# Group statistics and the channel gate inside the attention stream: blockwise transposes on VectorE in place of one-column matmuls

## The chip, the cores and the metric

The kernel runs on one core of a Trainium2 chip. Its engines each work through a queue of their own in order: TensorE (PE, with its weight loads shown apart as PEld), VectorE (DVE), ScalarE (ACT), GpSimd (POOL) and SyncE (SP, which issues DMAs here). The metric is device time in microseconds (us) for one execution.

## The reference

The input is x of shape (4, 64, 96, 96). Layer 0 normalizes x in 32 groups of two channels, runs an attention whose weights are sigmoids (no softmax), adds the residual, and multiplies each channel by a gate. Layer 1 normalizes again and applies a spectral convolution.

```python
def _gn(v, G=32, eps=1e-5):            # groups of C/G = 2 channels
    g = v.reshape(B_, G, C_ // G, H_, W_)
    m, s = mean(g, (2, 3, 4)), var(g, (2, 3, 4))
    return (g - m) / sqrt(s + eps)

# layer 0, on u = _gn(x):
energy = einsum('bcn,bcm->bnm', Q, K);  att = sigmoid(energy)
out = einsum('bcm,bnm->bcn', V, att) + u
mlp = lambda f: relu(f @ ca_w1.T) @ ca_w2.T      # 64 -> 4 -> 64
scale = sigmoid(mlp(mean(out)) + mlp(max(out)))
x = x + out * scale
# layer 1: low modes of rfft2(_gn(x)) times complex weights, irfft2, plus x
```

## The kernel before

**Layout.** One image is a tile `xs[p]` of 128 partitions by 4608 columns: partition 64h + c holds channel c of the upper (h = 0) or lower (h = 1) half of the picture. A group of two channels therefore lies in four partitions: c, c+1, 64+c, 64+c+1.

**The stream.** The attention of all four images is one long stream of 5184 tiles. A tile is 128 keys by 512 queries: an energy matmul (`energies`, L551) writes one PSUM bank, ScalarE takes the sigmoid into SBUF (`sigmoids`, L572), and a value matmul (`attend`, L589) adds the result to an accumulator bank. An image has 9 query blocks of 144 tiles each; when a block ends, VectorE adds the accumulator to `xs` and takes sums and maxima (L595, L597).

Tiles go in bursts. In round t TensorE does the energies of burst t+1, then the values of tiles whose sigmoids are done; ScalarE does the sigmoids of burst t+1 in two instructions, of three or four banks and the rest. PSUM has 8 banks: one accumulates, seven hold a burst. A round at a block's edge needs both accumulators, and so has a burst of six.

**Side work** is placed by a planner that runs while the kernel is built (L801 to L879), and it writes out the order on TensorE, VectorE and ScalarE by hand:

- `alone[t]`: a step with its own small matmul. It takes the free accumulator bank, so the burst planned in that round has six tiles instead of seven (`few = crossing or t in alone`, L865). It stands between the energies and the values on TensorE, and ahead of the sigmoids on ScalarE's queue.
- `together[t]`: a step that borrows banks of the burst just read (the projections `values_of`, L460, and the way back from the spectrum).
- `ends[t]`: VectorE work or DMA issues at the end of a round. The steps of a round that comes just before an edge are put off until after it (`put_off`, L909).
- `follow(own, step, wait, since)` adds a step to a chain that is handed out in order: `own` True makes it `alone`, None puts it in `ends`, a number in `together`; `wait` is the least number of rounds after the step before it.

**The three places that the change touches:**

1. `stats_of(p)` (L599) for the images p = 1, 2, 3 while image p-1 is attended: nine `bn_stats`, `bn_aggr` (`first`), and then two matmuls against the constant `pav`, which averages over the four partitions of a group: the mean (`shared`, L154), and the variance with the spread of the means (`third`, L165). `second` and `third` are `alone` in the rounds three after the edges m = 4 and m = 5 (L817). GpSimd then raises to the power -1/2 (L168).
2. `after(p)` (L612), the gate of image p, begins at the edge where its attention ends: `means` in `ends`, `hidden` (two matmuls with `w1`, L629 and L630) and `gates` (a matmul with `w2`, L636, a sum on VectorE, L639, and a sigmoid on ScalarE, L640) `alone`, two rounds apart.
3. `stats_steps(p)` (L282), the same statistics for layer 1 of images 0 to 2: two `alone` rounds in the chain after the last `along_w`.

That is 18 `alone` rounds. The chain also holds 9 + 3 + 16 others (`along_w`, `along_h`, `mixing`) that the change leaves.

At the end of round t = edge and in the next ones VectorE also has the last projections of the next image (L487, L477, then its splits), which TensorE needs to be read from PSUM, and copies of its keys (`kT<-stage`, L523), which wait for DMAs issued by GpSimd (L521) six rounds before.

Of the kernel before, what the change touches and what calls it, by code (L numbers as in the profile page):

```python
# [33 lines left out]
F32 = mybir.dt.float32  # L34
# [6 lines left out]
P = 128  # L41
# [6 lines left out]
KW = 16  # L48
# [24 lines left out]
QK = 4 * C8  # L73
FIRST = {"wq": P, "wk": P, "wv": C + 2 * C8, "pav": P, "bq": 1, "bk": 1, "low": 2, "nhalf": 1,
         "bv": P, "bqk": 2 * C8}
SECOND = {"w1": R, "w2": P, "fw": 2 * KW, "fh": 4 * KH, "gh": 2 * H, "gw": 4 * W}
PLACE, _at = {}, 0
for _name, _n in {**FIRST, **SECOND}.items():
    PLACE[_name] = slice(_at, _at + _n)
# [12 lines left out]
def tile_kernel(ctx: ExitStack, tc: tile.TileContext, x, cst, late, spec, out):  # L92
# [41 lines left out]
    def group_stats(stats, bank, name):  # L134


        mv = small.tile([P, 2], F32, tag=f"mv_{name}", name=f"mv_{name}", bufs=1)
        mr = small.tile([P, 2], F32, tag=f"mr_{name}", name=f"mr_{name}", bufs=1)
        t = small.tile([P, 1], F32, tag=f"t_{name}", name=f"t_{name}", bufs=1)
        d = small.tile([P, 1], F32, tag=f"d_{name}", name=f"d_{name}", bufs=1)  # L140

        def first():
            nc.vector.bn_aggr(mv, stats.rearrange("p s k -> p (s k)"))

        def second():
            shared()
            offset()
            spread_out()

        pm = []  # L150

        def shared():
            pm.append(bank(f"pm_{name}"))
            nc.tensor.matmul(pm[0][:, 0:1], pav, mv[:, 0:1], start=True, stop=True)  # L154

        def offset():
            nc.vector.tensor_copy(mr[:, 0:1], pm[0][:, 0:1])
            nc.vector.tensor_tensor(d, mv[:, 0:1], mr[:, 0:1], ALU.subtract)

        def spread_out():  # L160
            nc.vector.scalar_tensor_tensor(t, d, d, mv[:, 1:2], ALU.mult, ALU.add)

        def third():
            pv = bank(f"pv_{name}")
            nc.tensor.matmul(pv[:, 0:1], pav, t, start=True, stop=True)  # L165
            ve = small.tile([P, 1], F32, tag="ve", name=f"ve_{name}")
# [5 lines left out]
        return mr, [first, second, third], mv  # L172

    def normalize(dst, src, mr):
        nc.vector.tensor_scalar(dst, src, mr[:, 0:1], mr[:, 1:2], ALU.subtract, ALU.mult)
# [64 lines left out]
    class Hidden(Mixing):  # L240
# [39 lines left out]
                    self.xd[s].rearrange("(k w) (h n c) -> n w h k c", k=4, n=NSQ, c=SQ)[n])  # L280

        def stats_steps(self, p):  # L282
            mr, steps, _ = group_stats(self.stats[p], self.bank, f"l1_{p}")
            return steps + [lambda: self.spread(p, mr)]

        def spread(self, p, mr):
# [117 lines left out]
    with tc.tile_pool(name="work", bufs=1) as work, \  # L404
# [16 lines left out]

        def bank_a(name):
            return banks[:, spare[0], :]

        projected = [None]
        attended = [None]
# [172 lines left out]
        def stats_of(p):  # L599

            stats = small.tile([P, NBLK, 6], F32, tag=f"stats0_{p}", bufs=1, name=f"stats0_{p}")
            mr, steps, mv = group_stats(stats, bank_a, f"l0_{p}")
# [9 lines left out]
        def after(p):  # L612

            f = small.tile([P, 2], F32, tag=f"f{p}", bufs=1, name=f"f_{p}")
            top = small.tile([C, 1], F32, tag=f"top{p}", bufs=1, name=f"top_{p}")
            hid = small.tile([R, 2], F32, tag=f"hid{p}", bufs=1, name=f"hid_{p}")
            gate = small.tile([P, 1], F32, tag=f"gate{p}", bufs=1, name=f"gate_{p}")

            def means():
                tot = small.tile([P, 1], F32, tag="tot", name=f"tot_{p}")  # L620
                nc.vector.tensor_reduce(f[:, 1:2], maxs[p], AX.X, ALU.max)
# [3 lines left out]
                nc.vector.tensor_scalar(f[:, 0:1], tot, 1.0 / HALF, None, ALU.mult)  # L625

            def hidden():
                ph = bank_a(f"ph_{p}")
                nc.tensor.matmul(ph[:R, 1:2], named("w1", C), f[:C, 1:2], start=True, stop=True)  # L629
                nc.tensor.matmul(ph[:R, 0:1], named("w1"), f[:, 0:1], start=True, stop=True)  # L630
                nc.vector.tensor_scalar(hid[:, 0:1], ph[:R, 0:1], 0.5, 0.0, ALU.mult, ALU.max)
                nc.vector.tensor_scalar(hid[:, 1:2], ph[:R, 1:2], 0.0, None, ALU.max)

            def gates():
                pg = bank_a(f"pg_{p}")
                projected[0] = nc.tensor.matmul(pg[:, 0:2], named("w2", R), hid,  # L636
                                                start=True, stop=True)
                gsum = small.tile([P, 1], F32, tag="gsum", name=f"gsum_{p}")
                nc.vector.tensor_reduce(gsum, pg[:, 0:2], AX.X, ALU.add)  # L639
                nc.scalar.activation(gate, gsum, AF.Sigmoid)  # L640

            return gate, [means, hidden, gates], f

        def warm(s, n=NB // 2):

# [38 lines left out]
        def end(t, step):  # L684
            ends.setdefault(t, []).append(step)
# [17 lines left out]
        def follow(own, step, wait=1, since=0):  # L703

            chain.append((own, step, wait, since))
# [7 lines left out]
                nc.gpsimd.dma_start(w, spec[NSLOT + i])  # L713

        l1 = Hidden(bank_a, lambda dst, src: nc.vector.tensor_copy(dst, src), work)  # L715
        l1.banks = lambda n: banks[:, spare[0]:spare[0] + n, :]
        places = {}

# [22 lines left out]

        def second_layer(p, first):

            gate, steps, _ = after(p)
            end(first, steps[0])
            for step in steps[1:]:
                follow(True, step, 2)
            apart = APART if p < HIDDEN - 1 else APART_LAST
            end(first + 3, lambda: l1.fetch(p, 0))
            for s in range(NSTRIP):  # L750
                end(first + 7 + apart * s, lambda s=s: l1.result(p, s, gate))
                end(first + 9 + apart * s, lambda s=s: l1.turned(p, s))
            for m in range(NSTRIP // 2):
                follow(True, lambda m=m: l1.along_w(p, m), 1, 15 + apart * (2 * m + 1))
            stats = l1.stats_steps(p)
            follow(None, stats[0])
            for step in stats[1:3]:
                follow(True, step, 2)
            follow(None, lambda: (stats[3](), home(p)), 2)
            follow(True, lambda: l1.along_h(p), 2)  # L760
            if p < HIDDEN - 1:
                return

            def room():
# [36 lines left out]
        while len(done) < len(sizes):  # L801
# [6 lines left out]
            if crossing:  # L808
                edges.add(t)
                p, m = (n - 1) // NBLK + 1, (n - 1) % NBLK + 1  # L810
                for i in range(4):
                    if p < B and m >= 6 and 4 * (m - 6) + i < NBLK:
                        end(t + 2 + i, stats0[p][1][4 * (m - 6) + i])
                    if p < B and 4 * (m - 1) + i <= NBLK:
                        end(t + 2 + i, stats0[p][0][4 * (m - 1) + i])
                if p < B and m in (4, 5):
                    alone[t + 3] = stats0[p][0][NBLK + m - 3]  # L817
                if p == B and 3 <= m < 6:
                    for s in (2 * m - 6, 2 * m - 5):
                        end(t + 2, lambda s=s: bring(s))  # L820
# [319 lines left out]
def _constants(l0):  # L1140
# [15 lines left out]
    def put(name, what, rows=slice(0, P)):  # L1156
        a[rows, PLACE[name]] = what
# [8 lines left out]
    for b in range(2):  # L1166
# [8 lines left out]
            a[:, at:at + C8] = l0[w][None, :]  # L1175
        a[rows, PLACE["w1"]] = l0["ca_w1"].T
        a[:R, PLACE["w2"].start + b * C:PLACE["w2"].start + (b + 1) * C] = l0["ca_w2"].T
    put("bv", np.tile(l0["bv"], 2)[None, :])
    put("pav", np.kron(np.ones((2, 2)), np.kron(np.eye(C // 2), np.full((2, 2), 0.25))))

# [65 lines left out]
```

## Time and profile before

| | |
|---|---|
| median of three runs | 3021.2 us (3020.45 to 3021.38) |
| the profiled execution | 3020.43 us, of which the span of its instructions is 3018.7 us |
| PE busy | 3000.9 us (99%) |
| ACT busy | 2406.6 us (80%) |
| DVE busy | 335.8 us (11%), 814 instructions |
| POOL busy | 145.0 us (5%) |
| granted TensorE clock | 0.999 |

The stream begins 18.9 us after the span's start; its last burst begins at 2957.0 us. What follows is the tail: layer 1 of the last image. In a timeline, a group of L551 matmuls begins a burst, and the time to the next such group is the length of the round. An energy matmul is one record; a value matmul and the small ones are two. Values are taken in pairs of tiles and halves of pairs, so that seven tiles of values show as x16 of L589 and six as x12 or x16.

### The profile page before, as it was taken

The page shows a single profiled execution, that of the slowest core. Times are in us where ns is not written, and L with a number is a line of the kernel's source. Part 1 is how long each engine was busy: PE and PEld are TensorE (multiplying, and loading weights), DVE is VectorE, ACT ScalarE, POOL GpSimd, SP SyncE. Part 2 cuts the span into 40 slices and gives each one's busy share as a digit, 9 for nine tenths or more (in the row PEclk, how much of TensorE's full clock was granted, in tenths as well). Part 3 has the DMA queues.
Part 4 walks back from the last instruction along what each step waited for, and adds up shares of the span by engine and source line. Part 5 has one row for each costly group of instructions (what it writes and reads, how often), then busy time and mean ns, then how long its engine had stood idle before and what let it go on. Part 6 is the DMA issues. An engine that isn't in the chain of part 4 may idle for free.

```text
span 3018.7 us, 44581 instructions
## 1 busy us (share of the span) xinstructions
PE 3000.9 (99%) x19360; PEld 1091.3 (36%) x19360; DVE 335.8 (11%) x814; ACT 2406.6 (80%) x1539; POOL 145.0 (5%) x295
## 2 busy tenths in 40 slices
PE   9999999999999999999999999999999999999998
PEld 3333333333333333333333333333333333333334
DVE  4100000002111000001311000000221110100104
ACT  5888888887887888888788888888788777777783
POOL 1100000004000000001300000000310000000000
PEclk9999999999999999999999999999999999999999
DMA  4000000002230000001322000000243243312224
GB/s 167 20 4 4 4 4 4 4 2 56 68 77 17 4 4 4 4 5 23 82 69 72 4 4 4 4 3 2 44 109 98 77 158 86 55 47 64 67 93 153
DMA packets 157267, 133.96 MB, mean 44 GB/s; under 512 B 118960, under 2 KB 123120, under 8 KB 156784
## 3 DMA queue, kind: packets, MB, share of 16 engines
q1 hardware_dynamic: 145152, 110.06, 13.5%
q0 software_dynamic: 11344, 19.69, 2.2%
q8 instruction: 152, 2.49, 0.3%
q10 hardware_dynamic: 576, 1.38, 0.1%
q14 instruction: 43, 0.35, 0.0%
HBM read 91.53 MB, written 38.73 MB: 43 GB/s over the span
## 4 chain that ended last, share of the span: by engine, by line
PE 98%; DVE 1%; DMA 0%; ACT 0%; issue 0%; SPq 0%; POOL 0%; DVEq 0%; ACTq 0%
PE banks L589 78%; PE banks L551 17%; PE banks L470 1%; PE banks L215 1%; PE banks L394 0%; PE pv L215 0%; PE banks L300 0%; PE banks L366 0%; DMA x<-in_x_dram 0%; PE banks L328 0%; ACT at L572 0%; PE pa L1007 0%; DVE xt L997 0%; PE banks L436 0%; DVE x L180 0%
## 5 line engine op out<-in xcount | busy, mean ns | idle before, releaser
L572 ACT ACTIVATE at<-banks 128x2048 f32<-128x2048 f32 (+1 forms) x1505 | 2388.9, 1638 | 548.2 <-PE banks L551 535.8
L589 PE MATMUL banks<-at,vT 128*64 128x512 f32 (+1 forms) x11780 | 2406.6, 548 | 0.0
L589 PEld LDWEIGHTS banks<-at,vT 128*64 128x64 f32 x11780 | 773.8, 136 | 1352.3 <-issue 1297.5
L551 PE MATMUL banks<-q,kT 32*128 32x512 f32 x5040 | 543.0, 452 | 0.3 <-ACT at L572 0.3
L551 PEld LDWEIGHTS banks<-q,kT 32*128 32x128 f32 x5040 | 223.6, 182 | 453.0 <-issue 331.4
L595 DVE SCALAR_TENSOR_TENSOR x<-banks,x 128x512 f32<-128x512 f32 x36 | 24.9, 692 | 1663.4 <-PE banks L589 1663.4
L521 POOL DMA_DIRECT2D stage<-qk x256 | 125.7, 499 | 937.7 <-DMA qk<-turned 927.1
L168 POOL TENSOR_TENSOR mr_l<-ve_l,cs 128x1 f32<-128x1 f32 x7 | 3.9, 556 | 1288.7 <-DVE ve_l L167 1288.7
L398 DVE TENSOR_TENSOR x<-banks,x 128x768 f32<-128x768 f32 x18 | 17.2, 958 | 212.3 <-PE banks L394 212.3
L470 PEld LDWEIGHTS banks<-cs,x 64*64 64x64 f32 x1152 | 22.6, 135 | 27.2 <-ACT at L572 25.6
L487 DVE TENSOR_TENSOR u<-banks,cs 128x128 f32<-128x128 f32 x35 | 10.2, 291 | 191.0 <-PE banks L470 191.0
L739 POOL DMA_DIRECT2D w_early<-in_spec_dram x12 | 6.4, 542 | 518.5 <-PE banks L394 357.7
L470 PE MATMUL banks<-cs,x 64*64 64x80 f32 (+1 forms) x1152 | 28.3, 236 | 0.0
L477 DVE TENSOR_TENSOR vT<-banks,cs 128x256 f32<-128x256 f32 x72 | 26.9, 415 | 0.0
L715 DVE COPY ae<-banks 128x512 f32<-128x512 f32 x9 | 6.2, 692 | 174.8 <-PE banks L300 128.8
L597 DVE TENSOR_REDUCE maxs<-x 128x1 f32<-128x512 f32 x36 | 24.7, 686 | 1.2
L715 DVE COPY ws<-banks 128x512 f32<-128x512 f32 x16 | 11.1, 692 | 116.8 <-PE banks L215 116.8
L603 DVE BATCH_NORM_STATS2 stats<-x 128x6 f32<-128x512 f32 x36 | 23.3, 681 | 4.3 <-DMA x<-in_x_dram 4.3
L180 DVE SCALAR_TENSOR_TENSOR x<-x,gate,old 128x768 f32<-128x768 f32 x18 | 18.2, 1009 | 17.5 <-DMA old<-in_x_dram 17.5
L508 DVE STREAM_TRANSPOSE turned<-t 128x384 f32<-128x384 f32 (+1 forms) x35 | 19.9, 568 | 1.4 <-DVE t L506 0.3
L551 PE MATMUL banks<-q_first,kT 32*128 32x512 f32 x144 | 16.6, 463 | 2.7 <-ACT at L572 1.8
L523 DVE CAST kT<-stage 128x256 fp32r<-128x256 f32 x64 | 16.0, 287 | 24.3 <-DMA stage<-qk 24.1
(144 smaller groups left out, 402.0 us busy)
## 6 DMA issues: line engine op xcount, KB each, us to landing
ws<-in_spec_dram SPq DMA_DIRECT2D x32, 512.0 KB
q<-qk SPq DMA_DIRECT2D x280, 32.0 KB
stage<-qk POOLq DMA_DIRECT2D x256, 32.0 KB, 1.9
out_dram<-x SPq DMA_DIRECT2D x20, 384.0 KB
x<-in_x_dram SPq DMA_DIRECT2D x9, 768.0 KB
old<-in_x_dram SPq DMA_DIRECT2D x18, 384.0 KB
x1d<-x SPq DMA_DIRECT2D x18, 384.0 KB
xd<-old SPq DMA_DIRECT2D x18, 384.0 KB
```

The costliest lines, as they stand in the source:

```text
L180: nc.vector.scalar_tensor_tensor(xs[p][:, cols], xs[p][:, cols], gate, old, ALU.mult, ALU.add)
L215: self.last = nc.tensor.matmul(pv[bass.ts(g, 32), :].rearrange("q (n k o) -> q n k o", n=SIDE, o=C)[:, :, k, :], self.ut[:, at:at + 32], s ...
L470: projected[0] = nc.tensor.matmul(pp[bass.ts(e, P // 2), b, 2 * a + h, :width], src[rows, a, h, bass.ts(e, P // 2)], named("wv")[rows, :wi ...
L477: nc.vector.tensor_tensor(vTs[p % 2][:, 8 * s:8 * s + 8, :].rearrange("p (a h b) m -> p b a h m", h=2, b=2)[:, b], pp[:, b, :, :C].rearran ...
L508: nc.vector.transpose(turned[:, k:].rearrange("p k a (m h) -> p (k a) h m", h=2), t[:, k:].rearrange("p k a h m -> p (k a) h m").bitcast(F32))
L521: nc.gpsimd.dma_start(come[bass.ts(r, QK), :], split[p][s // 2][:, r // 2, bass.ts(s % 2, NB // 2)])
L551: nc.tensor.matmul(banks[:, bank_of(i), :], kT[r:r + 32, i % TILES // 8, i // 4 % 2, :], ask[i // TILES][r:r + 32, :], start=True, stop=True)
L572: nc.scalar.activation(at[:, of:of + n, :], banks[:, bank:bank + n, :], AF.Sigmoid)
L589: attended[0] = nc.tensor.matmul(acc[half, cols], vTs[n // NBLK % 2][:, j, :], at[:, place(2 * pair + b), cols], start=(j == 0), stop=(j = ...
L595: nc.vector.scalar_tensor_tensor(blk, acc, 1.0, blk, ALU.mult, ALU.add, accum_out=sums[p][:, m:m + 1])
L597: mark[0] = nc.vector.tensor_reduce(maxs[p][:, m:m + 1], blk, AX.X, ALU.max)
L603: each = [lambda s=s: nc.vector.bn_stats(stats[:, s, :], xs[p][:, bass.ts(s, NB)]) for s in range(NBLK)]
```

## The change

The steps listed above lose their matmuls. In the stream, `group_stats` is replaced by `group_stats_across`: `first` as before; `halves` brings the lower half's 64 partitions over and averages the two halves, then transposes a 64x64 patch in 32x32 blocks, so that channels lie along the row; `neighbours` averages even and odd channels there, writes the result to both, and transposes back; `third` copies the result to both halves. The gate's `after(p, True)` does its two small products as elementwise products with constants laid out for it (`w1r`, `w2r`, 36 more columns of the constant tile), sums along rows, and transposes. All scratch space is one `ae` tile (two buffers, shared with `along_w` and others).

The steps are put in `ends`, one a round, instead of `alone`. The statistics of layer 0 come right after the last `bn_stats`. The first image's statistics (before the stream) and the last image's gate and layer-1 statistics (after it) stay as they were.

```diff
+    def group_stats_across(stats, name, scratch):
+        def halves():
+            of, line, _, _ = places()
+            other, gap = place(7 * SQ, 7 * SQ + 2, False), place(7 * SQ + 2, 7 * SQ + 3, False)
+            nc.vector.memset(of, 0.0)
+            nc.vector.tensor_copy(other, mv[C:])
+            nc.vector.tensor_tensor(of[:, :, 0], mv[:C], other, ALU.add)
+            nc.vector.tensor_tensor(gap, mv[:C, 0:1], other[:, 0:1], ALU.subtract)
+            nc.vector.tensor_scalar(of[:, :, 0], of[:, :, 0], 0.5, None, ALU.mult)
+            nc.vector.tensor_scalar(gap, gap, 0.5, None, ALU.mult)
+            nc.vector.scalar_tensor_tensor(of[:, 1, 0:1], gap, gap, of[:, 1, 0:1], ALU.mult, ALU.add)
+            nc.vector.transpose(line, of)
+        def neighbours():
             ...   (even and odd columns averaged, nine instructions, the last a transpose)
+        def third():
+            for half in range(2):
+                rows = bass.ts(half, C)
+                nc.vector.tensor_copy(mr[rows, 0:1], line[:, 0, 0:1])
+                nc.vector.tensor_scalar(ve[rows], line[:, 1, 0:1], GN_EPS, None, ALU.add)
+            nc.gpsimd.tensor_tensor(mr[:, 1:2], ve, nhalf, ALU.pow)
+        return mr, [first, halves, neighbours, third], mv
...
         def stats_steps(self, p):
-            mr, steps, _ = group_stats(self.stats[p], self.bank, f"l1_{p}")
+            mr, steps, _ = group_stats_across(self.stats[p], f"l1_{p}", self.scratch)
...
+            def pooled():
+                means()
+                nc.vector.tensor_copy(top, f[C:, 0:1])
+                nc.vector.tensor_tensor(top, f[:C, 0:1], top, ALU.add)
+                nc.vector.tensor_scalar(f[:C, 0:1], top, 0.5, None, ALU.mult)
+                wide, lines = pairs(0), pairs(2 * SQ)
+                nc.vector.tensor_copy(wide, f[:C].unsqueeze(2).to_broadcast([C, 2, SQ]))
+                nc.vector.transpose(lines, wide)
+            def squeezed():
             ...   (product with w1r, sums, relu, spread over 128 partitions, transpose: 11 instructions)
+            def excited():
+                nc.vector.tensor_tensor(line[:, :R], line[:, :R], named("w2r"), ALU.mult)
+                nc.vector.tensor_reduce(gsum, line[:, :R], AX.X, ALU.add)
+                nc.scalar.activation(gate, gsum, AF.Sigmoid)
...
         def second_layer(p, first):
-            gate, steps, _ = after(p)
-            end(first, steps[0])
-            for step in steps[1:]:
-                follow(True, step, 2)
+            gate, steps, _ = after(p, True)
+            for i, step in enumerate(steps):
+                end(first + i, step)
...
-            stats = l1.stats_steps(p)
-            follow(None, stats[0])
-            for step in stats[1:3]:
-                follow(True, step, 2)
-            follow(None, lambda: (stats[3](), home(p)), 2)
+            for step in l1.stats_steps(p):
+                follow(None, step)
+            follow(None, lambda: home(p))
...
-                    if p < B and 4 * (m - 1) + i <= NBLK:
+                    if p < B and 4 * (m - 1) + i < len(stats0[p][0]):
                         end(t + 2 + i, stats0[p][0][4 * (m - 1) + i])
-                if p < B and m in (4, 5):
-                    alone[t + 3] = stats0[p][0][NBLK + m - 3]
```

More of the change, by code (lines that the diff above doesn't have):

```diff
@@ L75 @@
          "bv": P, "bqk": 2 * C8}
-SECOND = {"w1": R, "w2": P, "fw": 2 * KW, "fh": 4 * KH, "gh": 2 * H, "gw": 4 * W}
+SECOND = {"w1": R, "w2": P, "w1r": SQ, "w2r": R, "fw": 2 * KW, "fh": 4 * KH, "gh": 2 * H, "gw": 4 * W}
 PLACE, _at = {}, 0
@@ L172, in group_stats, with place, places, first @@
         return mr, [first, second, third], mv
+    def group_stats_across(stats, name, scratch):
+        mv = small.tile([P, 2], F32, tag=f"mv_{name}", name=f"mv_{name}", bufs=1)
+        mr = small.tile([P, 2], F32, tag=f"mr_{name}", name=f"mr_{name}", bufs=1)
+        room = []
+        def place(first, last, pair=True):
+            if not room:
+                room.append(scratch(name))
+            of = room[0][:C, first:last]
+            return of.rearrange("p (k n) -> p k n", k=2) if pair else of
+        def places():
+            return [place(0, 2 * SQ), place(2 * SQ, 4 * SQ), place(4 * SQ, 6 * SQ),
+                    place(6 * SQ, 7 * SQ, False)]
+        def first():
+            nc.vector.bn_aggr(mv, stats.rearrange("p s k -> p (s k)"))
+        def halves():
[10 more added lines that the diff above has]
+        def neighbours():
+            _, line, both, gaps = places()
+            even, odd = (line.rearrange("p k (g e) -> p k g e", e=2)[:, :, :, e] for e in range(2))
+            to = both.rearrange("p k (g e) -> p k g e", e=2)
+            for e in range(2):
+                nc.vector.tensor_tensor(to[:, :, :, e], even, odd, ALU.add)
+                nc.vector.tensor_tensor(gaps.rearrange("p (g e) -> p g e", e=2)[:, :, e],
+                                        even[:, 0], odd[:, 0], ALU.subtract)
+            nc.vector.tensor_scalar(both, both, 0.5, None, ALU.mult)
+            nc.vector.tensor_scalar(gaps, gaps, 0.5, None, ALU.mult)
+            nc.vector.tensor_tensor(gaps, gaps, gaps, ALU.mult)
+            nc.vector.tensor_tensor(both[:, 1], both[:, 1], gaps, ALU.add)
+            nc.vector.transpose(line, both)
+        def third():
+            _, line, _, _ = places()
+            ve = small.tile([P, 1], F32, tag="ve", name=f"ve_{name}")
+            for half in range(2):
[4 more added lines that the diff above has]
+        return mr, [first, halves, neighbours, third], mv
@@ L423, in bank_a, with scratch @@
             return banks[:, spare[0], :]
+        def scratch(name):
+            return work.tile([P, NB], F32, tag="ae", bufs=2, name=f"ae_{name}")
         projected = [None]
@@ L601, in stats_of @@
             stats = small.tile([P, NBLK, 6], F32, tag=f"stats0_{p}", bufs=1, name=f"stats0_{p}")
-            mr, steps, mv = group_stats(stats, bank_a, f"l0_{p}")
+            if p == 0:
+                mr, steps, mv = group_stats(stats, bank_a, f"l0_{p}")
+            else:
+                mr, steps, mv = group_stats_across(stats, f"l0_{p}", scratch)
             each = [lambda s=s: nc.vector.bn_stats(stats[:, s, :], xs[p][:, bass.ts(s, NB)])
@@ L610, in tile_kernel, with after @@
         maxs = [small.tile([P, NBLK], F32, tag=f"maxs{p}", bufs=1, name=f"maxs_{p}") for p in range(B)]
-        def after(p):
+        def after(p, across=False):
             f = small.tile([P, 2], F32, tag=f"f{p}", bufs=1, name=f"f_{p}")
@@ L640, in gates, with place, pairs @@
                 nc.scalar.activation(gate, gsum, AF.Sigmoid)
-            return gate, [means, hidden, gates], f
+            if not across:
+                return gate, [means, hidden, gates], f
+            room = []
+            def place(first, last, rows=C):
+                if not room:
+                    room.append(scratch(f"gate_{p}"))
+                return room[0][:rows, first:last]
+            def pairs(first):
+                return place(first, first + 2 * SQ).rearrange("p (k n) -> p k n", k=2)
@@ new lines, in pooled @@
+            def pooled():
[7 more added lines that the diff above has]
+            def squeezed():
+                wide, lines = pairs(0), pairs(2 * SQ)
+                sums_of, hid_in = place(6 * SQ, 6 * SQ + 2), place(6 * SQ + 2, 6 * SQ + 4, SQ)
+                of = place(6 * SQ + 4, 6 * SQ + 5, P)
+                spread, line = place(4 * SQ, 5 * SQ, P), place(5 * SQ, 6 * SQ, P)
+                nc.vector.tensor_tensor(
+                    wide, lines, named("w1r", C).unsqueeze(1).to_broadcast([C, 2, SQ]), ALU.mult)
+                nc.vector.tensor_reduce(sums_of, wide, AX.X, ALU.add)
+                nc.vector.tensor_copy(hid_in, sums_of[SQ:])
+                nc.vector.tensor_tensor(hid_in, sums_of[:SQ], hid_in, ALU.add)
+                nc.vector.tensor_scalar(hid_in, hid_in, 0.0, None, ALU.max)
+                nc.vector.tensor_reduce(of[:SQ], hid_in, AX.X, ALU.add)
+                for q in range(1, P // SQ):
+                    nc.vector.tensor_copy(of[bass.ts(q, SQ)], of[:SQ])
+                nc.vector.tensor_copy(spread, of.to_broadcast([P, SQ]))
+                nc.vector.transpose(line, spread)
@@ L644, in warm @@
+            def excited():
+                line = place(5 * SQ, 6 * SQ, P)
+                gsum = small.tile([P, 1], F32, tag="gsum", name=f"gsum_{p}")
+                nc.vector.tensor_tensor(line[:, :R], line[:, :R], named("w2r"), ALU.mult)
+                nc.vector.tensor_reduce(gsum, line[:, :R], AX.X, ALU.add)
+                nc.scalar.activation(gate, gsum, AF.Sigmoid)
+            return gate, [pooled, squeezed, excited], f
         def warm(s, n=NB // 2):
@@ L715, in tile_kernel @@
         l1 = Hidden(bank_a, lambda dst, src: nc.vector.tensor_copy(dst, src), work)
+        l1.scratch = scratch
         l1.banks = lambda n: banks[:, spare[0]:spare[0] + n, :]
@@ L1177, in _constants @@
         a[:R, PLACE["w2"].start + b * C:PLACE["w2"].start + (b + 1) * C] = l0["ca_w2"].T
+        a[rows, PLACE["w2r"]] = l0["ca_w2"]
+    for q in range(P // SQ):
+        at = q * SQ % C
+        for r in range(SQ):
+            a[q * SQ + r, PLACE["w1r"]] = l0["ca_w1"][r % R, at:at + SQ]
     put("bv", np.tile(l0["bv"], 2)[None, :])
```

## The prediction

> **What bounds the kernel now.** I read the page first: busy shares, then the chain, then the costliest groups.
>
> ```profile
> PE 3000.9 (99%) x19360; PEld 1091.3 (36%) x19360; DVE 335.8 (11%) x814; ACT 2406.6 (80%) x1539; POOL 145.0 (5%) x295
> PE 98%; DVE 1%; DMA 0%; ACT 0%; issue 0%; SPq 0%; POOL 0%; DVEq 0%; ACTq 0%
> L572 ACT ACTIVATE at<-banks 128x2048 f32<-128x2048 f32 (+1 forms) x1505 | 2388.9, 1638 | 548.2 <-PE banks L551 535.8
> ```
>
> TensorE is the chain, and ScalarE mostly waits for energies. So the change is worth what it takes from TensorE's queue. How much that is, a share cannot say; the TensorE timeline of single rounds can. First a plain burst of six, then two `alone` rounds of statistics with a round of seven between:
>
> ```profile
> 994.63 0.73 PE L551 MATMUL banks<-q,kT 32*128 32x512 f32 x6
> 995.30 2.80 PE L589 MATMUL banks<-at,vT 128*64 128x512 f32 x12
> 998.02 0.74 PE L551 MATMUL banks<-q,kT 32*128 32x512 f32 x7
> ...
> 936.12 0.73 PE L551 MATMUL banks<-q,kT 32*128 32x512 f32 x6
> 936.78 0.38 PE L154 MATMUL banks<-mv_l,cs 128*128 128x1 f32 x2
> 937.10 2.80 PE L589 MATMUL banks<-at,vT 128*64 128x512 f32 x12
> 939.82 0.74 PE L551 MATMUL banks<-q,kT 32*128 32x512 f32 x7
> 940.49 3.23 PE L589 MATMUL banks<-at,vT 128*64 128x512 f32 x16
> 943.65 0.73 PE L551 MATMUL banks<-q,kT 32*128 32x512 f32 x6
> ```
>
> From energies to energies: 3.39 us for six tiles, 3.70 with the one-column matmul, 3.82 for seven. These repeat to about 0.01 us over the stream, so rounds can be counted and priced. Next, ScalarE at a gate (image 2), with VectorE's instruction that it waits for:
>
> ```profile
> 2212.24 3.22 ACT L572 ACTIVATE at<-banks 128x2048 f32<-128x2048 f32 x2 [0.65 <-ACT at L572]
> 2216.51 0.20 ACT L640 ACTIVATE gate<-gsum 128x1 f32<-128x1 f32 x1 [1.05 <-DVE gsum L639]
> 2216.62 6.31 ACT L572 ACTIVATE at<-banks 128x2048 f32<-128x2048 f32 x4
> ...
> 2216.31 0.16 DVE L639 TENSOR_REDUCE gsum<-banks 128x1 f32<-128x2 f32 x1 [6.22 <-PE banks L636]
> ```
>
> The gate stands ahead of the next burst's sigmoids, waits for VectorE, which waits for TensorE's small matmul; the sigmoids start late and the round after takes 4.19 us instead of 3.82.
>
> **The change, part by part.** The two built programs' instruction order gives 752 bursts before and 749 after, 21 small matmuls fewer and 147 VectorE instructions more (17 for each of six statistics, 15 for each of three gates).
>
> *Removed, TensorE.* Twelve statistics rounds take 3.70 us, six of the first kind 3.74 on average, against 3.387 for a plain six: 6 x 0.354 + 6 x 0.316 = 4.0 us. Three `hidden` rounds take 3.633: 3 x 0.246 = 0.7. The three `gates` rounds with the round after each take 7.57, 7.92 and 7.58, against 3.387 + 3.822 = 7.21: 0.36 + 0.71 + 0.37 = 1.4. Together 6.1 us.
>
> *Removed, rounds.* 18 tiles move into fuller bursts. A tile of values costs 0.429 us wherever it stands (a round of six with eight tiles of values takes 4.245, so (4.245 - 3.387) / 2). What a round costs beyond its values is 3.822 - 7 x 0.429 = 0.82. Three rounds fewer: 2.5 us. The last burst has six tiles instead of three, so its energies take a second pass of four, about 0.2 (0.82 holds two such passes and their fill; between 0 and 0.4). Net 2.3 us.
>
> *Removed, uneven rounds.* After some edges a burst of seven tiles is computed while only six tiles of values are ready. Then ScalarE's 3.22 us do not fit:
>
> ```profile
> 1639.62 0.74 PE L551 MATMUL banks<-q,kT 32*128 32x512 f32 x7
> 1640.29 2.79 PE L589 MATMUL banks<-at,vT 128*64 128x512 f32 x12
> 1643.02 1.00 PE L551 MATMUL banks<-q,kT 32*128 32x512 f32 x7
> ```
>
> The next energies take 1.00 instead of 0.73: 0.27 lost. This happens 11 times apart from the gates; in the new order there are 6 such places. 5 x 0.27 = 1.35 us. This rests on where edges fall in rounds, so I bound it by 0 and 2.
>
> *Added, VectorE.* Rows for such instructions (128x1 to 128x9 elements) are 0.12 to 0.22 us, and the five of `means` run at 0.14 each start to start. I take 0.17, since most new ones follow each other's results; 0.14 and 0.22 are the ends. The few on 64x64 patches are near the 128x64 rows (0.19 a cast, 0.23 a sum of two). 147 x 0.17 = 25 us on an engine that is idle for 2680. `halves` (8 instructions, 1.4 us) and `neighbours` (9, 1.5) stand in rounds with no other VectorE work that TensorE needs; a strip of `result` there already takes 3.0 us (1.0 + 0.98 + 2 x 0.53) unnoticed. They cost nothing while a round's 3.82 us covers them.
>
> At the gate it is tighter:
>
> ```profile
> 2204.75 0.15 DVE L621 TENSOR_REDUCE f<-maxs 128x1 f32<-128x9 f32 x1
> 2205.31 0.15 DVE L625 TENSOR_SCALAR f<-tot 128x1 f32<-128x1 f32 x1
> 2207.20 0.29 DVE L487 TENSOR_TENSOR u<-banks,cs 128x128 f32<-128x128 f32 x1 [1.73 <-PE banks L470]
> 2209.51 0.46 DVE L523 CAST kT<-stage 128x256 fp32r<-128x256 f32 x2
> ```
>
> `pooled` adds five instructions after 2205.46: 0.85 us into 1.73 of idleness, so the projections behind it, whose banks TensorE needs, are not late. `squeezed` follows the key copies at 2209.97: 11 + 2 instructions, gsum at about 2212.2 (2211.8 to 2212.8). ScalarE has the gate after the sigmoids of its round, then seven tiles and ending at 2208.80 + 3.22 = 2212.02; the next sigmoids could start at 2212.43. So the gate falls into the gap, or pushes the sigmoids by up to 0.7. Before, 0.57 late (2216.62 against 2215.45 + 0.60) cost 0.36. I take 0.1 for each of three gates, bounds 0 and 0.7: 0.3 us.
>
> *Moved, other queues.* GpSimd's power instruction and SyncE's weight loads after `home` keep their order; `along_h` comes one round nearer to the last `along_w`, but its data left at 931.55 and it ran at 959.5, so 28 us become 24. The 36 constant columns ride on one load before the stream. The scratch takes a buffer of `ae` in turn; the copies out of it were issued rounds before. All at nothing, covered by rounds of 3.8 us.
>
> The sum: -6.1 - 2.3 - 1.35 + 0.3 = -9.5 us. Against the profiled execution's 3020.43 that is 3010.9; the median of the runs is 0.8 above it, so 3011.7.
>
> **A rule against the change.** The row is 0.14 us for each small instruction in `means`. The Trainium skill, "VectorE: DVE Perf Modes", section "Rules for kernel authors", says to minimize the count of chained VectorE operations and calls a reduction along partitions not possible on that engine. By it, 147 more operations in place of 21 matmuls would be a loss, up to their 20 to 25 us if VectorE were the bound. The trace has VectorE at 11% and TensorE at 99%, and the transposes bring the partitions into rows; I go by the trace.
>
> **Rivals.**
>
> *The gate stays late.* If the new instructions take 0.35 us each, as the whole latency of a dependent one might, gsum comes at 2214.5, the sigmoids start 2.2 us late, and 2 us are lost at each gate: 6 in all, 3017.4, within 0.2% of before. For it: 13 dependent instructions in a row. Against: L621 to L625, partly dependent on each other too, show 0.08 to 0.19 between starts.
>
> *Only the matmuls go.* If the rounds saved come back as late sigmoids (ScalarE is busy 3.22 of 3.82 us in a round of seven, and there are now more of seven) 6.1 - 0.3 remain: 3015.4. Against: 592 rounds of seven follow each other at 3.82, bound by TensorE.
>
> *VectorE stands before a DMA with the gate behind it.* Ahead of `squeezed` are key copies that wait for DMAs of GpSimd's queue. If those land late, VectorE, then ScalarE, then TensorE stop. This ends slower than before:
>
> ```profile
> 2189.72 3.91 POOL L521 DMA_DIRECT2D stage<-qk  x8 [4.31 <-DMA qk<-turned]
> ```
>
> Issued by 2193.6, landing 1.9 us later by the page, against 2209.97: 14 us to spare; at image 1 it is 11 (1466.81 + 3.91 + 1.9 against 1483.50). It breaks even if the data come 3.4 us after VectorE asks, at each gate (9.5 / 3, with 0.2 of slack), thus over 13 us later than now; it is over 0.2% slower at 5.4. At 6 each: 3029.
>
> **How the numbers follow.** 0.2% is 6.0 us, about what a measurement of this kernel can tell from no change. Forecast 0.80; gate late 0.08; matmuls only 0.06; VectorE behind a DMA, or another wait of its kind, 0.06. The forecast lies under 3015.2, and half of the second rival's 0.06: faster 0.83. Slower by 0.2%: 0.05 of the last. Same: 0.12. Range: the bounds of the parts give -9.5 - 0.65 - 0.3 - 0.2 = about -10.7 to -9.5 + 1.35 + 1.8 + 0.2 = -6.2, which is 3010.5 to 3015; I add the runs' own spread below (3009.5) and reach above to the first rival (3017).
>
> **What would show it.** The chain still TensorE at 98%; 749 groups of energies; no rounds of 3.70 or 3.63 us; the round after the gate at 3.82 and ScalarE without idle time "DVE gsum" above 0.3 us in the stream; VectorE busy about 25 us more. I am wrong if rounds of seven grow anywhere, above all just after the edges at about 750, 1475 and 2195 us, or if key copies show long waits for their DMA ahead of gsum.

## The result, and the profile after

| | before | after |
|---|---|---|
| median of nine runs each | 3021.2 us (3019.31 to 3023.37) | 3012.88 us (3010.46 to 3014.48) |
| ratio, 95% interval | | 0.9973 (0.9965 to 0.9981) |
| the profiled execution | 3020.43 us | 3014.48 us |
| its span | 3018.7 us | 3012.7 us |
| bursts of energies | 752 | 749 |
| start to the second burst | 26.4 us | 28.4 us |
| second burst to the last | 2930.64 us | 2921.17 us |
| last burst to the end | 61.6 us | 63.1 us |

The changed kernel is faster by 8.3 us between the medians, 0.27% (by the interval of the ratio, 5.7 to 10.6 us). The page of the changed kernel, in the order of the lines shown before:

```profile
PE 2994.6 (99%) x19366; PEld 1091.2 (36%) x19366; DVE 355.8 (12%) x961; ACT 2405.5 (80%) x1534; POOL 144.9 (5%) x295
PE 98%; DVE 1%; ACT 0%; DMA 0%; issue 0%; SPq 0%; POOL 0%; DVEq 0%; ACTq 0%
L632 ACT ACTIVATE at<-banks 128x2048 f32<-128x2048 f32 (+1 forms) x1500 | 2387.9, 1642 | 543.4 <-PE banks L611 531.5
```

TensorE is the chain as before, and VectorE is busy for 20.0 us more with 147 instructions more. (Line numbers move: energies are L611, sigmoids L632, values L649 now.)

The two spans differ by 6.0 us only, because the start happened to be slower in the second profile. Its second burst begins 2.1 us later: 0.95 us of that lie ahead of the first burst (which begins at 19.82 instead of 18.87), and 1.1 us between the first burst and the second, where the TensorE clock stood at half for 6.8 us instead of 3.4. So I compare from the second burst on: 2992.28 us before, 2984.27 after, 8.0 us less. That part repeats well. The same changed kernel, run again later, took 2921.19 us from the second burst to the last instead of 2921.17.

The timeline of ScalarE and VectorE at the gate of image 2, in the changed kernel:

```profile
2205.26 3.22 ACT L632 ACTIVATE at<-banks 128x2048 f32<-128x2048 f32 x2 [1.06 <-PE banks L611]
2209.11 0.20 ACT L749 ACTIVATE gate<-gsum 128x1 f32<-128x1 f32 x1 [0.64 <-DVE gsum L748]
2209.22 3.20 ACT L632 ACTIVATE at<-banks 128x2048 f32<-128x2048 f32 x2
...
2203.83 0.29 DVE L547 TENSOR_TENSOR u<-banks,cs 128x128 f32<-128x128 f32 x1 [0.66 <-PE banks L530]
2206.52 0.22 DVE L732 TENSOR_TENSOR ae_gate<-ae_gate,cs 64x64 f32<-64x64 f32 x1
2208.92 0.16 DVE L748 TENSOR_REDUCE gsum<-ae_gate 128x1 f32<-128x4 f32 x1
```

VectorE still waits 0.66 us for the projections, so `pooled` (1.0 us) fits into the idleness ahead of them. From the start of `squeezed` to the end of gsum are 2.56 us. The gate then comes at 2209.11, just when the next sigmoids would start (0.60 us after their energies of 2208.46 is usual, thus 2209.06). They start 0.76 us after the energies. The TensorE timeline shows that nothing is lost:

```profile
2204.64 0.74 PE L611 MATMUL banks<-q,kT 32*128 32x512 f32 x7
2208.46 0.73 PE L611 MATMUL banks<-q,kT 32*128 32x512 f32 x7
2212.28 0.74 PE L611 MATMUL banks<-q,kT 32*128 32x512 f32 x7
```

Both rounds take 3.82 us. What did come anew is elsewhere in the stream:

```profile
831.12 0.74 PE L611 MATMUL banks<-q,kT 32*128 32x512 f32 x6
834.52 0.73 PE L611 MATMUL banks<-q,kT 32*128 32x512 f32 x6
835.18 1.07 PE L357 MATMUL banks<-xT,cs 96*32 96x512 f32 x8
838.91 0.74 PE L611 MATMUL banks<-q,kT 32*128 32x512 f32 x7
842.73 0.50 PE L611 MATMUL banks<-q,kT 32*128 32x512 f32 x4
843.59 0.51 PE L611 MATMUL banks<-q,kT 32*128 32x512 f32 x3 [0.35 <-ACT at L632]
847.18 0.74 PE L611 MATMUL banks<-q,kT 32*128 32x512 f32 x7
...
837.78 1.02 ACT L632 ACTIVATE at<-banks 128x1024 f32<-128x1024 f32 x1 [0.77 <-PE banks L649]
840.32 6.33 ACT L632 ACTIVATE at<-banks 128x2048 f32<-128x2048 f32 x4 [1.52 <-PE banks L649]
```

A round of six at an edge (831.12) is followed by one with the step `along_w` (834.52). Two rounds later the energies come in two pieces, and the round takes 4.45 us instead of 3.82. ScalarE had started 1.41 us after the energies of 838.91: by the profile it waited for values (L649), which were still to read the slots of `at` that it writes. This happens here and at 1565.8 us; before, it happened once, at 2378 us.

### The profile page after: what moved, and what is told of

The parts are those of the page before. It is cut to its first block, busy times and chain, and to the rows that moved or that the text cites. A ratio compares the mean times of both kernels' runs of the same rounds, so it can differ in the third digit from the quotient of the medians.

```text
span 3012.7 us, 44733 instructions
## 1 busy us (share of the span) xinstructions
PE 2994.6 (99%) x19366; PEld 1091.2 (36%) x19366; DVE 355.8 (12%) x961; ACT 2405.5 (80%) x1534; POOL 144.9 (5%) x295
## 4 chain that ended last, share of the span: by engine, by line
PE 98%; DVE 1%; ACT 0%; DMA 0%; issue 0%; SPq 0%; POOL 0%; DVEq 0%; ACTq 0%
PE banks L649 78%; PE banks L611 17%; PE banks L530 1%; PE banks L272 1%; PE banks L451 0%; PE pv L272 0%; PE banks L357 0%; PE banks L756 0%; PE banks L423 0%; ACT at L632 0%; PE banks L385 0%; DMA x<-in_x_dram 0%; PE pa L1112 0%; DVE xt L1102 0%; PE banks L496 0%
## 5 line engine op out<-in xcount | busy, mean ns | idle before, releaser
L632 ACT ACTIVATE at<-banks 128x2048 f32<-128x2048 f32 (+1 forms) x1500 | 2387.9, 1642 | 543.4 <-PE banks L611 531.5
L649 PE MATMUL banks<-at,vT 128*64 128x512 f32 (+1 forms) x11828 | 2406.6, 547 | 0.0
L649 PEld LDWEIGHTS banks<-at,vT 128*64 128x64 f32 x11828 | 777.5, 136 | 1360.7 <-issue 1304.7
L611 PE MATMUL banks<-q,kT 32*128 32x512 f32 x5040 | 539.3, 452 | 0.7 <-ACT at L632 0.7
L611 PEld LDWEIGHTS banks<-q,kT 32*128 32x128 f32 x5040 | 222.6, 182 | 443.8 <-issue 339.4
L611 PE MATMUL banks<-q_first,kT 32*128 32x512 f32 x144 | 16.8, 471 | 2.5 <-ACT at L632 1.8
```

The lines of the kernel that those rows point to most:

```text
L611: nc.tensor.matmul(banks[:, bank_of(i), :], kT[r:r + 32, i % TILES // 8, i // 4 % 2, :], ask[i // TILES][r:r + 32, :], start=True, stop=True)
L632: nc.scalar.activation(at[:, of:of + n, :], banks[:, bank:bank + n, :], AF.Sigmoid)
L649: attended[0] = nc.tensor.matmul(acc[half, cols], vTs[n // NBLK % 2][:, j, :], at[:, place(2 * pair + b), cols], start=(j == 0), stop=(j = ...
```

## The experiments

All are timed against the kernel before on their own chip. The stream is the time from the second burst to the last, the tail from there to the end; both are from one profile.

| kernel | median, us | before, same chip | second burst | stream | tail | last two together |
|---|---|---|---|---|---|---|
| before | | | 26.37 | 2930.64 | 61.64 | 2992.28 |
| after | 3012.88 | 3021.2 | 28.43 | 2921.17 | 63.10 | 2984.27 |
| after, again | 3012.21 | 3020.89 | 26.09 | 2921.19 | 63.18 | 2984.37 |
| gate alone | 3017.02 | 3021.7 | 26.37 | 2926.85 | 62.10 | 2988.95 |
| statistics alone | 3016.07 | 3021.7 | 24.91 | 2925.18 | 61.89 | 2987.06 |
| rounds of six kept | 3016.97 | 3021.7 | 27.37 | 2927.33 | 63.11 | 2990.45 |
| none after an edge | 3010.5 | 3021.7 | 26.27 | 2919.95 | 63.59 | 2983.54 |
| gate slower by 12 | 3023.99 | 3020.81 | 25.46 | 2931.18 | 63.90 | 2995.08 |
| statistics slower | 3013.84 | 3020.81 | 26.04 | 2921.25 | 63.63 | 2984.88 |
| gate slower by 6 | 3015.97 | 3020.89 | 26.09 | 2924.53 | 63.49 | 2988.03 |
| by 12, sigmoid later | 3012.37 | 3020.89 | 26.00 | 2921.20 | 64.57 | 2985.77 |
| both improvements | 3010.49 | 3020.89 | 27.23 | 2919.89 | 63.88 | 2983.77 |

The stream repeats to a few hundredths where the programs agree in it. The tail of kernels with the same last burst of six tiles spreads from 63.1 to 64.6 us, so differences of a microsecond in the last column are read from the stream where that is possible.

### The gate alone

```diff
-                mr, steps, mv = group_stats_across(stats, f"l0_{p}", scratch)
+                mr, steps, mv = group_stats(stats, bank_a, f"l0_{p}")     (the l1 statistics likewise,
...                                                       and the alone rounds of both as before)
```

> Only the gate is moved to VectorE; all statistics keep their matmuls and their own rounds. Measured from the second burst of energies to the end (the start varies with the granted clock), before is 2992.3 us and the changed kernel 2984.3. Theory (cost is TensorE's small matmuls, the late sigmoids at the gate, and 0.82 us a round): the hidden and gates rounds give 0.7 + 1.4, one round fewer (751) 0.8, so 2.9 less than before: 2989.4, with 0.6 to either side for uneven rounds. Rival (the gate's late sigmoids were a small part, the gain is in the statistics): 1.5 less or nothing, 2991 to 2992.

Measured: 2988.95 from the second burst on, 3.3 us less than before; ratio 0.9985 (0.9976 to 0.9995). The twelve rounds with a statistics matmul stay, 3.70 us on average. This lies inside the theory's 2.9 give or take 0.6, and is twice the rival's 1.5.

### The statistics alone

```diff
-            gate, steps, _ = after(p, True)
-            for i, step in enumerate(steps):
-                end(first + i, step)
+            gate, steps, _ = after(p)
+            end(first, steps[0])
+            for step in steps[1:]:
+                follow(True, step, 2)
```

> Only the twelve statistics steps are moved to VectorE; the gate keeps its matmuls and its two rounds. From the second burst to the end, theory: 4.0 for the twelve rounds' matmuls, two rounds fewer (750) 1.6, less 0.2 for the second pass of energies in the last burst: 5.4 less than before, 2986.9, with 0.8 to either side for uneven rounds; the rounds after the gates still take about 4.18 us. Rival (gate and statistics are not additive, since each alone round only shifts the edges): about the whole 8 us here already, 2984.

Measured: 2987.06, 5.2 us less than before; ratio 0.9984 (0.9975 to 0.9993). The rounds after the gates take 4.19, 4.19 and 4.17 us. The two parts together give 3.3 + 5.2 = 8.5 us, the whole change 8.0: they add up within what uneven rounds and the tail move.

### The rounds of six kept, but empty

```diff
             for i, step in enumerate(steps):
                 end(first + i, step)
+            for _ in range(2):
+                follow(True, lambda: None, 2)
...
-            for step in l1.stats_steps(p):
+            for i, step in enumerate(l1.stats_steps(p)):
+                if i in (1, 3):
+                    follow(True, lambda: None)
                 follow(None, step)
...
+                if p < B and m in (4, 5):
+                    alone[t + 3] = lambda: None
```

> The changed kernel, with the 18 rounds of six tiles kept at their old places and empty. The bursts are then those of before, 752 with the same edges, and only the small matmuls and their waits are gone. Theory (6.1 us lie in the matmuls and the gate's wait, the rest in rounds): 6.1 less than before from the second burst on, 2986.2, and every formerly alone round at 3.39. Rival (the time is in the number of bursts, TensorE hides the matmuls): 2990 to 2992.

Measured: 2990.45, so 1.8 us less than before, where 6.1 was expected; by medians 4.7 less (ratio 0.9985, 0.9975 to 0.9994). The bursts have the sizes of before, apart from shifts by one round at layer 1's steps, so each round can be set against its counterpart. The TensorE timeline around the round that had the first matmul of image 1:

```profile
361.32 0.73 PE L611 MATMUL banks<-q,kT 32*128 32x512 f32 x6
361.98 2.80 PE L649 MATMUL banks<-at,vT 128*64 128x256 f32 x16
364.71 0.74 PE L611 MATMUL banks<-q,kT 32*128 32x512 f32 x7
```

It takes 3.39 us, 0.31 less than before. The twelve statistics rounds lose 0.30 to 0.34 each and the three `hidden` rounds 0.24, which is 4.5 us and confirms that term: the small matmuls were not hidden, although the 1.8 us of the sum lie where the rival had them. The expectation failed at the gate. ScalarE's and TensorE's timelines at image 1, in this kernel:

```profile
1485.04 0.20 ACT L749 ACTIVATE gate<-gsum 128x1 f32<-128x1 f32 x1 [0.97 <-DVE gsum L748]
1485.15 3.20 ACT L632 ACTIVATE at<-banks 128x2048 f32<-128x2048 f32 x2
...
1487.41 0.51 PE L611 MATMUL banks<-q,kT 32*128 32x512 f32 x3
1488.40 0.51 PE L611 MATMUL banks<-q,kT 32*128 32x512 f32 x3 [0.49 <-ACT at L632]
```

The rounds after the edge are of six tiles here, so ScalarE asks for the gate earlier than in the changed kernel, and VectorE is as late as there. The gate costs 0.77 us at image 1, 0.4 at image 2 and nothing at image 0, nearly as much as before (of 1.4 us, 0.3 are saved). The rest lies in rounds of the way back (5.01 us at 2464, 5.41 at 2802; 1.5 us in the stream) and in the tail (1.5 us), where the chain of work that ended last shows a DMA that takes 2.21 us in the kernel before:

```profile
2994.06 3.70 DMA vd<-w_early
```

Whether this kernel or this execution made those waits was not settled. The profiled execution was the slowest of its ten, 3019.60 us against a median of 3016.97, which points at the execution: the 4.7 us by medians are close to 4.5 for the rounds and 0.3 for the gates, though the interval of the ratio (1.8 to 7.6 us) is too wide to show it. The experiment holds for the 15 rounds; for the sum it is inconclusive.

### No step with matmuls right after an edge

```diff
                     if t < max(ready[0] + wait, started[0] + since):
                         break
+                    if own is True and t - 1 in edges:
+                        break
```

> The changed kernel, with a planner that does not put a step with its own matmuls in the round right after a block's edge. The changed kernel has two rounds of 4.45 us (at 843 and 1566 us), each two rounds after such a pair of six-tile bursts, where the sigmoids of a seven-tile burst wait. Theory (the pair causes it): both go, 1.25 less than the changed kernel, 2983.0 from the second burst on. Rival (it is the way back along W itself, or VectorE's strips beside it): the long rounds move with the steps and the time stays at 2984.3.

Measured: the stream is 1.22 us shorter than the changed kernel's, and the two rounds of 4.45 us are gone; ratio to before 0.9964 (0.9951 to 0.9976). With the tail, which was 0.5 longer in this profile, 2983.54. TensorE's timeline there:

```profile
832.40 0.73 PE L611 MATMUL banks<-q,kT 32*128 32x512 f32 x7
836.22 0.73 PE L611 MATMUL banks<-q,kT 32*128 32x512 f32 x6
836.88 1.07 PE L357 MATMUL banks<-xT,cs 96*32 96x512 f32 x8
840.60 0.74 PE L611 MATMUL banks<-q,kT 32*128 32x512 f32 x7
844.43 0.73 PE L611 MATMUL banks<-q,kT 32*128 32x512 f32 x7
848.25 0.74 PE L611 MATMUL banks<-q,kT 32*128 32x512 f32 x7
```

With a round of seven between the edge and `along_w`, all that follow take 3.82 us. The step is still there, one round later. So the pair of sixes was the cause, and not the step itself.

### A slower gate, by twelve and by six instructions

```diff
                 nc.vector.tensor_reduce(gsum, line[:, :R], AX.X, ALU.add)
+                for _ in range(12):        (6 in the second kernel)
+                    nc.vector.tensor_scalar(gsum, gsum, 1.0, None, ALU.mult)
                 nc.scalar.activation(gate, gsum, AF.Sigmoid)
```

> The changed kernel with twelve more dependent VectorE instructions (times one) on the gate's sum ahead of its sigmoid, about 2.2 us at 0.18 each. Theory (the gate stands in ScalarE's queue, and now comes just in time): the next sigmoids start 2.2 to 2.4 us late at each of three gates and TensorE loses about 2.1 each, 6.4 in all: 2990.7 from the second burst on. Rival (ScalarE, busy 80%, catches up before TensorE needs it): below 1 us, 2984 to 2985.

Measured: 10.0 us more than the changed kernel in the stream, and slower than the kernel before (ratio 1.0016, 1.0006 to 1.0026). The theory is right in kind; the size had something beside it. TensorE's timeline at the gate of image 2, with twelve:

```profile
2211.54 0.73 PE L611 MATMUL banks<-q,kT 32*128 32x512 f32 x7
2216.48 0.50 PE L611 MATMUL banks<-q,kT 32*128 32x512 f32 x4 [1.05 <-ACT at L632]
2217.82 0.50 PE L611 MATMUL banks<-q,kT 32*128 32x512 f32 x3 [0.84 <-ACT at L632]
2218.26 4.92 PE L649 MATMUL banks<-at,vT 128*64 128x512 f32 x16
```

The next seven tiles of energies wait twice for ScalarE, and then the values come. Three windows around it, with busy times, granted clock (the third column from the end) and DMA:

```profile
2215.00:2218.90 3.90, 2.01 (x14) 0.72 (x13) 2.75 (x4) 3.90 (x3) 1.43 (x3) 1.00 0.65 218
2218.90:2222.40 3.50, 3.50 (x12) 0.98 (x8) 0.00 (x0) 2.09 (x2) 2.01 (x5) 0.51 0.88 223
2222.40:2226.00 3.60, 3.60 (x27) 1.38 (x25) 2.32 (x4) 2.27 (x2) 0.00 (x0) 1.00 0.86 180
```

At image 0 the two rounds around the stop take 4.92 and 4.93 us, 2.2 lost: the 2.2 us of added work. At images 1 and 2 TensorE stands still about as long, and then the granted clock is at half for 3.4 us: seven tiles of values take 4.92 instead of 3.23. There 1.7 to 1.9 us more are lost than at image 0.

> Six dependent VectorE instructions more on the gate's sum (1.1 us) instead of twelve. With twelve, TensorE lost 2.2 us at each gate, and at two of three the granted clock then stood at half for 3.4 us, some 1.8 more. Theory (a late gate costs its lateness less 0.15, and the half clock comes only after a longer stop): about 1.1 lost at each gate, 3.3 in all, and no half clock in the stream. Rival (any stop of TensorE brings the half clock): 1.1 + 1.8 each, 8 to 9 in all.

Measured with six: 3.34 us more in the stream, one round of 4.92 us at each gate, and no half clock. That is the theory's 3.3. In both kernels the sigmoids at the gate are later than usual by 0.2 us more than TensorE loses (2.4 late and 2.2 lost at image 0 with twelve, 1.3 and 1.1 at image 2 with six): that is the slack.

### Slower statistics

```diff
+            for _ in range(15):
+                nc.vector.tensor_scalar(of, of, 1.0, None, ALU.mult)
             nc.vector.transpose(line, of)     (in neighbours likewise, with both)
```

> The changed kernel with fifteen more VectorE instructions on 64x64 patches (times one) in each of the steps halves and neighbours, 3.0 to 3.5 us a step, twelve steps, some 40 us of VectorE time. Theory (nothing waits for the statistics soon, VectorE is idle there): no more than 0.5 us more than the changed kernel, 2984.3 to 2984.8 from the second burst on. Rival (work on VectorE delays the reading of accumulators or key copies): up to 3 us a step where it collides, 2990 and above.

Measured: 0.08 us more in the stream, ratio to before 0.9976 (0.9967 to 0.9985). VectorE is busy for 33.5 us more than in the changed kernel (389.3 against 355.8). The statistics' VectorE work is free as it stands, and would be at more than twice its length.

### Slower by twelve, and the sigmoid one round later

```diff
+                for _ in range(12):
+                    nc.vector.tensor_scalar(gsum, gsum, 1.0, None, ALU.mult)
-                nc.scalar.activation(gate, gsum, AF.Sigmoid)
+            def opened():                     (in ends of the next round)
+                nc.scalar.activation(gate, sums_ready[0], AF.Sigmoid)
```

> The twelve additional instructions as before, but ScalarE's sigmoid for the gate is given out one round later. Theory (what costs is the place in ScalarE's queue, not the VectorE work): the loss of 10 us is gone, from the second burst to the end as the changed kernel, 2984 to 2986, and no half clock in the stream. Rival (VectorE, later by 2.2 us there, holds up TensorE's banks or keys): most of the 10 us remains.

Measured: stream 2921.20, that of the changed kernel; the 10 us are gone. ScalarE's timeline:

```profile
2206.63 3.22 ACT L632 ACTIVATE at<-banks 128x2048 f32<-128x2048 f32 x2 [0.60 <-PE banks L611]
2209.73 0.20 ACT L756 ACTIVATE gate<-gsum 128x1 f32<-128x1 f32 x1
2210.45 3.22 ACT L632 ACTIVATE at<-banks 128x2048 f32<-128x2048 f32 x2 [0.51 <-PE banks L611]
```

The gate waits for nobody and lies in the gap before the next energies. So it is the place in ScalarE's queue that decides, not the amount of VectorE work.

### Both improvements, beside the changed kernel

> The changed kernel once more, beside its variants on the same chip: 0.9973 of before, 3012 to 3014 us; 2984.3 from the second burst on, give or take 1.5 for waits in the tail.

Measured: median 3012.21, ratio 0.9969 (0.9958 to 0.998), and 2984.37 from the second burst on, as expected.

```diff
+                    if own is True and t - 1 in edges:
+                        break
...            (and the gate's sigmoid in a step opened, one round later)
```

> The changed kernel with both: no step with its own matmuls right after an edge, and the gate's sigmoid one round later. Theory: 1.25 us less than the changed kernel from the first, nothing from the second, as the gate now costs nothing already. Rival (a gate that comes just in time is late in some executions): 2 us or more less than the changed kernel in the median.

Measured: stream 2919.89, 1.30 us less than the changed kernel on the same chip, as the theory has it. Medians 3010.49 and 3012.21; ratios to before 0.9966 (0.9954 to 0.9978) and 0.9969. By total time the two are not told apart; by the stream the 1.30 us are from the edges, as in the kernel with that rule alone (1.22), and the later sigmoid adds nothing that can be measured. It is the fastest kernel here beside that one (3010.5).

## Why the prediction was right

Forecast 3011.7, measured 3012.88; -9.5 us forecast, -8.3 measured between medians, -8.0 in the profile from the second burst on. The mechanism was right in its main part, the matmuls and the gate's wait. Of the 1.5 us between -9.5 and -8.0, the uneven rounds are 1.35 and the fewer rounds about 0.4 counted too much; the gate's loss of 0.3, which did not come, goes the other way. That errors of both signs met makes the sum look a little better than its terms.

- **The small matmuls, 6.1 us: confirmed.** With the bursts kept and the matmuls gone, fifteen rounds each fell by 0.30 to 0.34 or 0.24 us, 4.5 us together where 4.7 was worked out. The gates' 1.4 are gone from the changed kernel: its rounds there take 3.82 us.
- **Three rounds fewer, 2.3 us net: consistent, and not shown by itself.** The number came as read from the instruction order. From the last burst to the end of its values TensorE takes 5.38 us before and 6.89 after; these 1.5 us are what three tiles of values (1.3) and the second pass of energies (0.2) had been priced at, and the rest of the tail is equal (56.3 and 56.2). What is left for this term is 8.0 - 6.1 = 1.9 us, by subtraction alone, 0.4 less than worked out. The kernel that was to separate rounds from matmuls was disturbed by its gate and its DMA waits.
- **Uneven rounds, 1.35 us: this term was wrong.** The predicted kind did become rarer (0.27 us at 11 places before, at four after). But I had counted only rounds of seven with six tiles of values. The new order brought two rounds of 4.45 us, 0.63 each, after an edge directly followed by a step with matmuls (before: one), and some ten rounds 0.06 to 0.12 late, whose cause I did not look for. Against the usual length of like rounds, late rounds apart from gates and start sum to about 4 us both before and after. So the term was worth about nothing, which is the lower bound that I had set for it.
- **The gate's new path, 0.3 us lost: it was 0.** The chain took 2.56 us where 2.2 was worked out: from start to start the 64x64 instructions, the copy over 128 partitions and the transpose took 0.22 to 0.26, and many small ones 0.19, not 0.17. So the sigmoids were late, by 0.16 us, but TensorE lost nothing by it: 0.2 us of slack covered it. The old gate shows the same slack (0.57 late, 0.36 lost).
- **VectorE's 25 us: 20.0, and free.** Taking the rule on the operation count as the bound would have meant a loss; the slower statistics show that there is room for 33.5 us more in their rounds.
- **The rivals.** "The gate stays late" is the mechanism that twelve instructions brought about; its price is as stated (2 us a gate) only until the clock halves. "Only the matmuls go" did not come: rounds of seven stay at 3.82 us. "VectorE before a DMA" did not come: key copies wait longer in total, but near the gates of the changed kernel each such wait begins 3.3 us or more after the gate's sigmoid.
- **The signs.** Two that I had named came the wrong way. ScalarE was to have no idle time "DVE gsum" above 0.3 us; it has 0.6 at each of three gates, and that costs nothing. No round of seven was to grow; the two of 4.45 us did.

The waits for DMAs and for gsum, of before and then of after:

```profile
DVE kT L523 <- DMA stage<-qk: 24.1, 11, 6.4
```

```profile
DVE kT L583 <- DMA stage<-qk: 38.8, 14, 8.3
ACT gate L749 <- DVE gsum L748: 1.9, 3, 0.6
```

Behind the gates the key copies wait for 4.6 us before and for 19.8 after; the rest lies at the start of the stream. Probably VectorE, no longer stopped by the gates' matmuls, comes to these copies sooner; that was not traced. The rounds there take 3.82 us, so TensorE loses nothing by it.

## What to carry to other kernels

On a saturated engine, price a small instruction by the round it stands in: here a one-column matmul cost 0.31 us, and the wait that the gate's matmul put into another engine's queue cost 0.36 to 0.71. Moving the work to an idle engine was free here, except where its result enters a queue that the busy engine depends on; look at that one place in the timeline, and give the consumer out a round later if it is close. When a planner lays out the order, taking steps away moves all edges: read the new order for what now stands side by side before counting on its round lengths.

## What the runs showed of the hardware

- In the middle of the stream, half clock followed stops of TensorE that were well under the length of the half-clock spell (3.4 us). With stops of 1.27 and 0.84 us within 2.6 us (image 1) and of 1.05 and 0.84 (image 2) the granted clock stood at half for the next 3.4 us; with 1.03 and 0.83 (image 0), or 0.83 alone (the kernel with six instructions, at all gates), it did not. The Trainium skill, "TensorE: Matmul & The Clock Gate", section "Why this matters for your kernels", advises against idle gaps above about 3 us. Here the measurement differs: stops of 2.11 and 1.89 us in sum, inside one spell's length, were followed by half clock, and stops of 1.86 were not. Where the bound lies, and whether the place of the stops counts beside their sum, was not settled.
- The start of the stream has no half clock, 3.4 us or 6.8 us of it in different profiles, of one kernel too (6.8 and 3.4 for the changed kernel). From the first burst to the second it takes 6.3 us with none (two profiles), 7.3 to 7.7 with 3.4 us (eight) and 8.6 with 6.8 us (two). These 2.3 us are a good part of the 4 us by which the nine executions of the changed kernel differ; its two fastest are those with a granted clock of 1.000.
